# A Mamba layer on Trainium2: decays leave PSUM two pairs ahead, inputs stay there and are weighted in place, and the next image's norm is spread over five blocks

## The chip, the cores and the metric

The kernel runs on one core of one Trainium2 chip (trn2). The core has five engines with a queue each: PE (TensorE, the matmuls), ACT (ScalarE), DVE (VectorE), POOL (GpSimd) and SP (SyncE, which issues the DMAs here). Each engine takes its queue strictly in order; semaphores join the queues. The metric is the device time of one execution in microseconds (us). Three runs of the kernel before took 8034.1, 8043.04 and 8058.09 us, a median of 8043.04.

## What is computed

Four layers over `x` of 4 images, 56 x 56 positions, 128 channels, all in float32. Layer 0 is a neighbourhood attention, layer 2 an additive attention and a mixture of experts, layer 3 an attention and a second mixture of experts. The change is in layer 1, a group norm and two Mamba blocks in a row on each image row (a sequence of 56 steps):

```python
x = x + _L1_conv_ref(_gn(x), ...)          # _gn: mean and variance over 32 groups of an image

def _mamba_block(h, in_w, cw, cb, xw, dtw, dtb, A_log, Dp, ow):
    xz = h @ in_w                           # 128 -> 2 x 256
    u, res = jnp.split(xz, 2, axis=-1)
    u = silu(causal_conv(u, cw) + cb)       # 4 taps along the sequence
    dbl = u @ xw
    dt, Bm, Cm = jnp.split(dbl, [DT_RANK, DT_RANK + D_STATE], axis=-1)
    delta = softplus(dt @ dtw + dtb)
    A = -jnp.exp(A_log)
    y = _selective_scan(u, delta, A, Bm, Cm, Dp)
    return y * silu(res) @ ow

def _selective_scan(u, delta, A, Bm, Cm, Dp):
    deltaA = jnp.exp(jnp.einsum('btd,dn->btdn', delta, A))      # the decays
    deltaBu = jnp.einsum('btd,btn->btdn', delta * u, Bm)        # the inputs
    # h = deltaA[t] * h + deltaBu[t];  y[t] = sum over n of h * Cm[t]
    return y + u * Dp
```

There are 256 channels with 16 states each, so 4096 recurrences for each position.

## The kernel before, in words

**Blocks.** An image is cut into 7 chunks of 8 rows (448 positions). A block is one chunk in one of the two Mamba layers `l`; `order` lists 4 x 14 = 56 of them: for each image, chunks 0 to 3 in layer 0, then in layer 1, then chunks 4 to 6 in layer 0, then in layer 1. So the last block of an image that reads the normed image is its eleventh, and the next image's first block comes three blocks later.

**Pairs.** A block has 16 pairs. A pair is 2 x 8 channels x 16 states on 128 partitions, for 448 positions each: tiles of 128 x 896. For every pair the kernel does this:

- decays, `select`: two matmuls (PE, L654) spread `delta` times `A` into the PSUM tile `a` (two banks, two buffers); ACT takes the exponential in place (L668);
- inputs, `select` and `inputs`: two matmuls (PE, L663) spread `du` = delta * u into the PSUM tile `u` (two banks, one buffer). In 11 pairs of 16, DVE multiplies it by `Bm` (tile `bc`) into the SBUF tile `dBu` (L678). In the 5 pairs of `BY_POOL`, ACT copies it to SBUF (L672) and POOL multiplies it there (L673), since POOL has no access to PSUM;
- the recurrence, `scan`: one DVE scan instruction (L685) reads `a` (PSUM) and `dBu` (SBUF) and writes `hs` (SBUF, 7 buffers). The decay at the first position of each row is made 0 by a huge `delta`. POOL then multiplies `hs` by `Cm` (L690);
- `sums`, for two pairs at a time, five steps later: matmuls (PE, L696) add the states into the PSUM tile `y` (one bank), which began with `Dp * u` (`skip`, L704).

After 8 pairs `y` is complete for half the channels; `gate` multiplies it by silu(res) on DVE (L711). `project` (L720 or L728) is the output matmul, and `pass_on` (L738 on ACT for layer 0, L744 on DVE for layer 1) hands the result to the next layer or adds it to `X`.

**What prepares a block.** `mamba_pre` does the convolution, the projections, softplus and silu for the next block during the 16 steps of the current one. Its matmuls share one PSUM bank, `m`, with `project` and the norm. ACT changes its function table on the way from exp to silu and back, and from exp to softplus and back: four table loads for a block.

**The order** is written by hand. One step `p` issues, on all queues: the list `first[p]`, `select(p + 1)`, `scan(p)`, `sums` on odd steps, the list `last[p]`, and `inputs(p + 2)`. `select(p + 1)` issues on PE the decays of pair p+1 and then the inputs' matmuls of pair p+2. So a decay is made one step ahead of its scan and the weighted input two steps ahead. PE takes matmuls on different 32-row groups at the same time: decays use two of the groups of 32 partitions, the inputs' matmuls of the next pair the other two.

**The norm of the next image**, `prepare_image` from `group_norm_steps`: 7 steps that transpose a chunk (PE, L184), take its statistics (DVE, L187) and copy it to SBUF (ACT, L188), then `mean`, `var` and the normalising multiplies. Six of the chunks fall in three steps (11, 12, 13) of the block that is three before the image's first; the seventh, `mean`, `var` and all multiplies (L211) in steps 11 and 12 of the block after that.

**PSUM** has 8 banks: `m` 1, `a` 2 x 2, `u` 2, `y` 1.

Of the kernel before, what the change touches and what calls it, by code (L numbers as in the profile page):

```python
# [39 lines left out]

BY_POOL = (0, 3, 6, 9, 12)
# [65 lines left out]
class Hybrid:  # L107
# [61 lines left out]
    def group_norm_steps(self, b, pool, psum, group, pad=0):  # L169


        nc = self.nc
# [3 lines left out]
        def transposed(c):  # L176
            if c == 0:
                got["xn"] = self.t(pool, [P, HW, pad + HW], "xnT")
                got["st"] = self.t(pool, [P, NCH, nc.vector.BN_STATS_DIM], "gn_st")
                if pad:  # L180
                    nc.gpsimd.memset(got["xn"][:, :, 0:pad], 0.0)
            ps = psum()
            for k in range(TC):
                nc.tensor.transpose(  # L184
                    ps[:, k * TP : (k + 1) * TP], self.X[b][:, TC * c + k, :], self.ident[:TP, :TP]
                )
            nc.vector.bn_stats(got["st"][:, c, :], ps[:, :CH])  # L187
            nc.scalar.copy(chunk(c), ps[:, :CH].rearrange("p (s t) -> p s t", t=HW))  # L188

        def mean():  # L190
            mv = self.t(pool, [P, 2], "gn_mv")
            nc.vector.bn_aggr(mv, got["st"])
            pm = psum()
            nc.tensor.matmul(pm[:, 0:1], group, mv[:, 0:1], start=True, stop=True)
            got["mean"] = mean = self.t(pool, [P, 1], "gn_mean")
            nc.vector.tensor_copy(mean, pm[:, 0:1])
            got["dev"] = dev = self.t(pool, [P, 1], "gn_dev")
            nc.vector.tensor_sub(dev, mv[:, 0:1], mean)
            nc.vector.tensor_mul(dev, dev, dev)
            nc.vector.tensor_add(dev, dev, mv[:, 1:2])  # L200

        def var():
            pv = psum()
            nc.tensor.matmul(pv[:, 0:1], group, got["dev"], start=True, stop=True)
            var = self.t(pool, [P, 1], "gn_var")
            nc.vector.tensor_copy(var, pv[:, 0:1])
            got["r"] = self.rstd(pool, var, [P, 1], 1e-5, "gn")

        def normed(cs):
# [7 lines left out]
            [bind(transposed, c) for c in range(NCH)] + [mean, var]  # L217
            + [bind(normed, cs) for cs in (range(0, 2), range(2, 4), range(4, NCH))]
        )

# [104 lines left out]
    def layer0(self):  # L325
# [5 lines left out]
        with ExitStack() as ctx:  # L331
# [31 lines left out]
            def norm_steps(b):  # L363
                got, steps = self.group_norm_steps(b, big, m, group)
# [228 lines left out]
    def layer1(self):  # L593
# [5 lines left out]
        with ExitStack() as ctx:  # L599
# [5 lines left out]
            ps_a = ctx.enter_context(tc.tile_pool(name="l1_a", bufs=2, space=PSUM))  # L605
            ps_u = ctx.enter_context(tc.tile_pool(name="l1_u", bufs=1, space=PSUM))
# [14 lines left out]
            pre, yg, A, U, V, HS, py = {}, {}, {}, {}, {}, {}, {}  # L621

            def prepare_image(b):

                got, steps = self.group_norm_steps(b, big, m, w["group"], DC - 1)
# [5 lines left out]
                def rest():  # L631
                    for step in steps[NCH + 2 :]:
                        step()
                    hand_over()

                return steps[: NCH + 2] + [rest]
# [9 lines left out]


            def select(p):
                if 0 <= p < n_pairs:
                    j, f, q, r0 = place(p)  # L650
                    A[p] = two_banks(ps_a, "a")
                    for k in range(2):
                        own = slice((r0 + k) * HD, (r0 + k + 1) * HD)
                        nc.tensor.matmul(  # L654
                            halves(A[p])[:, k], w["A"][own, order[j][2], f, q, :], pre[j]["delta"][own, f],
                            start=True, stop=True,
                        )
                if p + 1 < n_pairs:
                    j, f, q, r0 = place(p + 1)
                    U[p + 1] = two_banks(ps_u, "u")  # L660
                    for k in range(2):
                        own = slice((r0 + k) * HD, (r0 + k + 1) * HD)
                        nc.tensor.matmul(  # L663
                            halves(U[p + 1])[:, k], w["pick"][own, q, :], pre[j]["du"][own, f],
                            start=True, stop=True,
                        )
                if 0 <= p < n_pairs:
                    nc.scalar.activation(A[p], A[p], AF.Exp)  # L668
                if p + 1 < n_pairs and (p + 1) % PAIRS in BY_POOL:
                    V[p + 1] = self.t(sm, [P, 2 * CH], "dBu", bufs=3)  # L670
                    v = halves(V[p + 1])
                    nc.scalar.copy(V[p + 1], U.pop(p + 1))  # L672
                    nc.gpsimd.tensor_mul(v, v, pre[j]["bc"][:, 0:1].to_broadcast([P, 2, CH]))  # L673

            def inputs(p):
                if p in U:
                    V[p] = self.t(sm, [P, 2 * CH], "dBu", bufs=3)
                    nc.vector.tensor_mul(  # L678
                        halves(V[p]), halves(U.pop(p)), pre[p // PAIRS]["bc"][:, 0:1].to_broadcast([P, 2, CH])
                    )  # L680


            def scan(p):
                flat = self.t(sm, [P, 2 * CH], "hs", bufs=7)
                nc.vector.tensor_tensor_scan(  # L685
                    flat, A.pop(p), V.pop(p), 0.0, op0=ALU.mult, op1=ALU.add
# [21 lines left out]
            def gate(j, f):  # L708
                if f == 0:
                    yg[j] = self.t(sm, [P, NHALF, CH], "yg", bufs=1)  # L710
                nc.vector.tensor_mul(yg[j][:, f], py.pop((j, f)), pre[j]["sres"][:, f])  # L711
# [38 lines left out]
            for j, block in enumerate(order):  # L750
                at = PAIRS * j
                if j and block[1:] == (0, 0):
                    for k, step in enumerate(prepare_image(block[0])):
# [1037 lines left out]
```

## Time and profile before

| what | us |
|---|---|
| median of three runs | 8043.04 |
| the profiled execution | 8038.93 |
| its span, first to last instruction | 8037.1 |
| layer 0 and the start, until the first scan | 637.4 |
| Mamba stage, first scan to start of the last | 637.4 to 3644.7 |
| layers 2 and 3 | about 3660 to 8037 |

Within the Mamba stage (the window 637 to 3646 us):

| group | count | mean ns | busy us |
|---|---|---|---|
| POOL `hs` times `Cm`, L690 | 895 | 2082 | 1840.0 |
| DVE scan, L685 | 896 | 2014 | 1795.2 |
| DVE `u` times `Bm`, L678 | 616 | 1078 | 664.0 |
| POOL `dBu` times `Bm`, L673 | 279 | 2084 | 581.3 |
| ACT exp, L668 | 896 | 906 | 811.3 |
| ACT copy of `u`, L672 | 279 | 911 | 254.1 |
| ACT table loads of L668, L804 and L835, four for a block | 225 | 1283 | 288.7 |
| DVE gate, L711 | 111 | 607 | 67.4 |

How to read a profile like this one: an engine's busy share over the whole span says little, since each layer has other limits; the window of the stage counts. A group's "idle before" is what its engine waited ahead of such an instruction, and the name behind the arrow is the instruction that ended the wait.

The starts of every sixteenth scan in the trace give the length of each block. 49 of the 55 blocks between the first and the last start of one last 52.3 us on average (49.6 to 53.6). The other six, the two ahead of the last block of each of the first three images, last 68.0 and 65.6 us: these are the ones with the norm of the next image in them.

### The profile page before, as it was taken

The page shows a single profiled execution, that of the slowest core. Times are in us where ns is not written, and L with a number is a line of the kernel's source. Part 1 is how long each engine was busy: PE and PEld are TensorE (multiplying, and loading weights), DVE is VectorE, ACT ScalarE, POOL GpSimd, SP SyncE. Part 2 cuts the span into 40 slices and gives each one's busy share as a digit, 9 for nine tenths or more (in the row PEclk, how much of TensorE's full clock was granted, in tenths as well). Part 3 has the DMA queues.
Part 4 walks back from the last instruction along what each step waited for, and adds up shares of the span by engine and source line. Part 5 has one row for each costly group of instructions (what it writes and reads, how often), then busy time and mean ns, then how long its engine had stood idle before and what let it go on. Part 6 is the DMA issues. An engine that isn't in the chain of part 4 may idle for free.

```text
span 8037.1 us, 106369 instructions
## 1 busy us (share of the span) xinstructions
PE 6835.5 (85%) x41037; PEld 2717.5 (34%) x41037; DVE 5818.5 (72%) x10093; ACT 5183.5 (64%) x5084; POOL 2975.3 (37%) x2077
## 2 busy tenths in 40 slices
PE   8878998999899999996777777777777779999999
PEld 4442333333333333332222222222222334444544
DVE  6777887888788888886777887887787764434434
ACT  4545565566565556655999899899989964333332
POOL 4547887888788888881000000000001000000000
PEclk9989998999899989998999899999989989999999
DMA  2000000000000000000000000000003101210000
GB/s 53 2 13 1 1 1 1 1 1 1 1 1 1 1 1 1 1 1 5 1 1 1 5 1 1 1 5 1 1 21 122 46 6 34 91 65 5 6 5 6
DMA packets 85494, 102.39 MB, mean 13 GB/s; under 512 B 21158, under 2 KB 50742, under 8 KB 84279
## 3 DMA queue, kind: packets, MB, share of 16 engines
q1 hardware_dynamic: 84985, 95.58, 4.0%
q8 instruction: 322, 5.28, 0.3%
q14 instruction: 187, 1.53, 0.1%
HBM read 85.28 MB, written 10.29 MB: 12 GB/s over the span
## 4 chain that ended last, share of the span: by engine, by line
PE 38%; ACT 17%; POOL 15%; issue 14%; DVE 10%; DMA 0%; SPq 0%; ACTq 0%; DVEq 0%; POOLq 0%
ACT th L1017 13%; POOL hs L690 10%; PE q L1563 7%; PE o L1574 7%; PE s L1028 6%; DVE th L1008 5%; POOL dBu L673 4%; PE o L1055 3%; PE a L654 2%; PE pe L1728 2%; PE m L792 2%; PE y L696 1%; PE u L663 1%; PE m L728 1%; POOL du L839 1%
## 5 line engine op out<-in xcount | busy, mean ns | idle before, releaser
L1017 ACT ACTIVATE th<-th 128x3136 f32<-128x3136 f32 (+12 forms) x1120 | 2294.2, 2094 | 202.5 <-DVE th L1008 147.7
L1008 DVE TENSOR_SCALAR th<-fT,g 128x784 f32<-128x784 f32 (+6 forms) x3920 | 1917.7, 556 | 492.1 <-PE s L1028 459.2
L1028 PE MATMUL s<-th,place 128*32 128x392 f32 (+7 forms) x14336 | 1488.1, 492 | 672.7 <-ACT th L1017 669.4
L685 DVE TENSOR_TENSOR_SCAN hs<-a,dBu 128x896 f32<-128x896 f32 x896 | 1795.2, 2014 | 274.5 <-ACT a L668 265.5
L690 POOL TENSOR_TENSOR hs<-hs,bc 128x896 f32<-128x896 f32 x896 | 1842.0, 2082 | 68.3 <-DVE hs L685 39.9
L668 ACT ACTIVATE a<-a 128x896 f32<-128x896 f32 x896 | 811.3, 906 | 790.7 <-PE u L663 604.9
L663 PE MATMUL u<-du,pick 32*128 32x448 f32 x3584 | 977.2, 619 | 96.8 <-ACT dBu L672 49.8
L654 PE MATMUL a<-delta,A_pick 32*128 32x448 f32 x3584 | 996.9, 605 | 7.0 <-DVE hs L685 6.1
L1028 PEld LDWEIGHTS s<-th,place 128*32 128x32 f32 (+1 forms) x14336 | 425.9, 111 | 1617.1 <-ACT th L1017 1089.5
L1046 POOL TENSOR_TENSOR e<-e,later 112x112 f32<-112x112 f32 x112 | 79.3, 708 | 2320.7 <-ACT e L1039 1680.8
L1568 ACT ACTIVATE e<-q,shift 128x448 f32<-128x448 f32 (+1 forms) x700 | 441.5, 634 | 729.8 <-PE q L1563 729.2
L678 DVE TENSOR_TENSOR dBu<-u,bc 128x896 f32<-128x896 f32 x616 | 664.0, 1078 | 164.6 <-PE u L663 163.4
L673 POOL TENSOR_TENSOR dBu<-dBu,bc 128x896 f32<-128x896 f32 x280 | 583.4, 2083 | 421.3 <-ACT dBu L672 421.2
L1574 PE MATMUL o<-e,xk 128*128 128x448 f32 (+1 forms) x1400 | 653.7, 549 | 25.7 <-ACT oT L1549 25.7
L1563 PE MATMUL q<-xT 128*128 128x448 f32 (+1 forms) x1400 | 653.8, 549 | 6.0 <-ACT e L1568 5.9
L1733 DVE SCALAR_TENSOR_TENSOR X<-pe,r_gate,X 112x128 f32<-112x128 f32 x896 | 314.1, 351 | 454.4 <-PE pe L1728 418.9
L654 PEld LDWEIGHTS a<-delta,A_pick 32*128 32x128 f32 x3584 | 313.7, 191 | 534.7 <-issue 246.2
L696 PE MATMUL y<-hs,sum 128*32 128x448 f32 x3584 | 446.8, 570 | 3.1 <-POOL hs L690 3.1
L1055 PE MATMUL o<-e,xa 112*128 112x392 f32 (+5 forms) x1024 | 427.5, 540 | 1.1 <-POOL e L1046 1.1
L663 PEld LDWEIGHTS u<-du,pick 32*128 32x128 f32 x3584 | 282.3, 191 | 331.1 <-DVE dBu L678 201.5
L1574 PEld LDWEIGHTS o<-e,xk 128*128 128x128 f32 (+1 forms) x1400 | 262.6, 191 | 310.0 <-issue 275.0
L1662 POOL MEMSET lc_xa<- 112x4 f32 x28 | 3.1, 110 | 893.2 <-DVE lc_xa L1656 625.8
(252 smaller groups left out, 7670.7 us busy)
## 6 DMA issues: line engine op xcount, KB each, us to landing
wide<-in_L_ffn_weight SPq DMA_DIRECT2D x64, 1024.0 KB
X<-in_x SPq DMA_DIRECT2D x8, 784.0 KB
out<-X SPq DMA_DIRECT2D x28, 224.0 KB
M<-wide SPq DMA_DIRECT2D x4, 784.0 KB
wide<-M SPq DMA_DIRECT2D x4, 784.0 KB
e_edge<-dtab SPq DMA_DIRECT2D x42, 49.0 KB
cw<-in_L_conv_conv_w SPq DMA_DIRECT2D x1, 1024.0 KB
c_h<-in_L_ffn_weight SPq DMA_DIRECT2D x16, 64.0 KB
```

The costliest lines, as they stand in the source:

```text
L654: nc.tensor.matmul(halves(A[p])[:, k], w["A"][own, order[j][2], f, q, :], pre[j]["delta"][own, f], start=True, stop=True,)
L663: nc.tensor.matmul(halves(U[p + 1])[:, k], w["pick"][own, q, :], pre[j]["du"][own, f], start=True, stop=True,)
L668: nc.scalar.activation(A[p], A[p], AF.Exp)
L673: nc.gpsimd.tensor_mul(v, v, pre[j]["bc"][:, 0:1].to_broadcast([P, 2, CH]))
L685: nc.vector.tensor_tensor_scan(flat, A.pop(p), V.pop(p), 0.0, op0=ALU.mult, op1=ALU.add)
L690: nc.gpsimd.tensor_mul(HS[p], HS[p], bc[:, 1:2].to_broadcast([P, 2, CH]))
L1008: nc.vector.tensor_scalar(th[i][:, blk, lo:hi], fT[j][:, lo:hi], im[order[j][0]]["g"][:, at : at + 1], None, op0=ALU.add,)
L1017: nc.scalar.activation(own, own, AF.Tanh)
L1028: nc.tensor.matmul(ps[j, J][QW * blk : QW * blk + rows, h, lo:hi], place[:, off : off + rows], z[:, blk, h * HALF + lo : h * HALF + hi], s ...
L1055: nc.tensor.matmul(po[j][:, h, lo:hi], im[b]["xa"][:, J, :], e[:, h * HALF + lo : h * HALF + hi], start=(J == 0), stop=(J == t + ((h + 1) ...
L1563: nc.tensor.matmul(ps[:n, :CH], xT[b][:, k : k + n], xT[b][:, c * CH : (c + 1) * CH], start=True, stop=True,)
L1574: nc.tensor.matmul(po[b, c], xk[b][:n, t, :], es.pop((b, c, t))[:n], start=(t == 0), stop=(t == N - 1))
```

## The change

- PSUM: `a` gets one buffer in place of two, `u` two in place of one.
- The decays are made two steps ahead: `select(p)` issues the decays of pair p+1 and the inputs' matmuls of pair p (each a pair later or earlier than before in the order). The exponential writes a new SBUF tile `E` (three buffers) and no longer works in place.
- The inputs stay in PSUM: DVE multiplies `u` by `Bm` in place, for all 16 pairs, one step ahead of the scan instead of two. `BY_POOL`, ACT's copy and POOL's multiply are gone, and so is `dBu`. The scan reads `E` from SBUF and `u` from PSUM.
- The gate becomes an ACT copy of `y` to SBUF and a POOL multiply; the first half is one step earlier, the second half at the end of step 3 and not at the start of step 4.
- `pass_on` moves from the start of its step (ahead of the scan) to the end.
- The norm of the next image: chunks in steps 11, 12, 13 of the blocks five and four before the image's first block, the seventh in step 11 of the third before; transposes at the end of a step, statistics and copy at the start of the next. Mean, variance and root are cut into six parts over steps 12 to 14 of the third block before, the multiplies in three parts and the handing over in steps 3, 5, 7 and 9 of the second. One DVE copy (of the variance) is gone. Layer 0 takes the same parts put together again as before.

```diff
-            ps_a = ctx.enter_context(tc.tile_pool(name="l1_a", bufs=2, space=PSUM))
-            ps_u = ctx.enter_context(tc.tile_pool(name="l1_u", bufs=1, space=PSUM))
+            ps_a = ctx.enter_context(tc.tile_pool(name="l1_a", bufs=1, space=PSUM))
+            ps_u = ctx.enter_context(tc.tile_pool(name="l1_u", bufs=2, space=PSUM))
...
+            def decays(p, to):
+                j, f, q, r0 = place(p)
+                for k in range(2):
+                    own = slice((r0 + k) * HD, (r0 + k + 1) * HD)
+                    nc.tensor.matmul(
+                        halves(to)[:, k], w["A"][own, order[j][2], f, q, :], pre[j]["delta"][own, f],
+                        start=True, stop=True,
+                    )
...
             def select(p):
+                if 0 <= p + 1 < n_pairs:
+                    t = two_banks(ps_a, "a")
+                    decays(p + 1, t)
                 if 0 <= p < n_pairs:
...
+                    V[p] = two_banks(ps_u, "u")
+                    spread_inputs(p, V[p])
+                if 0 <= p + 1 < n_pairs:
+                    E[p + 1] = self.t(sm, [P, 2 * CH], "E", bufs=3)
+                    nc.scalar.activation(E[p + 1], t, AF.Exp)
+
+            def inputs(p):
                 if 0 <= p < n_pairs:
-                    nc.scalar.activation(A[p], A[p], AF.Exp)
-                if p + 1 < n_pairs and (p + 1) % PAIRS in BY_POOL:
-                    V[p + 1] = self.t(sm, [P, 2 * CH], "dBu", bufs=3)
-                    v = halves(V[p + 1])
-                    nc.scalar.copy(V[p + 1], U.pop(p + 1))
-                    nc.gpsimd.tensor_mul(v, v, pre[j]["bc"][:, 0:1].to_broadcast([P, 2, CH]))
-
-            def inputs(p):
-                if p in U:
-                    V[p] = self.t(sm, [P, 2 * CH], "dBu", bufs=3)
+                    v = halves(V[p])
                     nc.vector.tensor_mul(
-                        halves(V[p]), halves(U.pop(p)), pre[p // PAIRS]["bc"][:, 0:1].to_broadcast([P, 2, CH])
+                        v, v, pre[p // PAIRS]["bc"][:, 0:1].to_broadcast([P, 2, CH])
                     )
...
-                    flat, A.pop(p), V.pop(p), 0.0, op0=ALU.mult, op1=ALU.add
+                    flat, E.pop(p), V.pop(p), 0.0, op0=ALU.mult, op1=ALU.add
...
-                nc.vector.tensor_mul(yg[j][:, f], py.pop((j, f)), pre[j]["sres"][:, f])
+                nc.scalar.copy(yg[j][:, f], py.pop((j, f)))
+                nc.gpsimd.tensor_mul(yg[j][:, f], yg[j][:, f], pre[j]["sres"][:, f])
...
-                    for k, step in enumerate(prepare_image(block[0])):
-                        add(last, at - (3 if k < 6 else 2) * PAIRS + 11 + k % 6 // 2, step)
-                add(last, at + 12, gate, j, 0)
-                add(first, at + PAIRS + 4, gate, j, 1)
+                    chunks, stats, norms = prepare_image(block[0])
+                    for k, (turn, take) in enumerate(chunks):
+                        to = at - (5 - k // 3) * PAIRS + 11 + k % 3
+                        add(last, to, turn)
+                        add(first, to + 1, take)
+                    to = at - 3 * PAIRS + 12
+                    for k, (where, step) in enumerate(zip((first, last) * 3, stats)):
+                        add(where, to + k // 2, step)
+                    for k, step in enumerate(norms):
+                        add(last, at - 2 * PAIRS + 3 + 2 * k, step)
+                add(last, at + 11, gate, j, 0)
+                add(last, at + PAIRS + 3, gate, j, 1)
                 add(last, at + PAIRS + 8, project, j)
-                add(first, at + PAIRS + 9, pass_on, j)
+                add(last, at + PAIRS + 9, pass_on, j)
...
-                inputs(p + 2)
+                inputs(p + 1)
```

In step p the order of the queues is now: `first[p]`; on PE the decays of pair p+2 and the inputs' matmuls of pair p+1; on ACT the exponential of pair p+2; on DVE `scan(p)`; `sums`; `last[p]`; on DVE the multiply of pair p+1.

## The prediction

> **What bounds the kernel now.** I read the slices of the span first, for the stage; then the stage's chain of waits; then its groups; then the engine sums of single blocks.
>
> The page's slices, 201 us each; slices 4 to 19 are the Mamba stage:
>
> ```profile
> PE   8878998999899999996777777777777779999999
> DVE  6777887888788888886777887887787764434434
> ACT  4545565566565556655999899899989964333332
> POOL 4547887888788888881000000000001000000000
> ```
>
> Three engines stand at 8 to 9 tenths and none is full, so waits between queues matter as much as any engine's sum. The change touches nothing that issues a DMA. The groups:
>
> ```profile
> L685 DVE TENSOR_TENSOR_SCAN hs<-a,dBu 128x896 f32<-128x896 f32 x896 | 1795.2, 2014 | 274.5 <-ACT a L668 265.5
> L690 POOL TENSOR_TENSOR hs<-hs,bc 128x896 f32<-128x896 f32 x896 | 1842.0, 2082 | 68.3 <-DVE hs L685 39.9
> L668 ACT ACTIVATE a<-a 128x896 f32<-128x896 f32 x896 | 811.3, 906 | 790.7 <-PE u L663 604.9
> L678 DVE TENSOR_TENSOR dBu<-u,bc 128x896 f32<-128x896 f32 x616 | 664.0, 1078 | 164.6 <-PE u L663 163.4
> ```
>
> POOL is busiest of the three where it works (16 x 2.08 + 5 x 2.08 + 2.08 = 45.8 us of a block of 52.3 us) and hardly waits; in the chain of this stage it holds 27.1% by L690 and 11.4% by L673. The scan's idle time is nearly all waiting for the exponential: the decay is made one step ahead, and each table change delays it. A plain block and one with the next image's norm (engine sums):
>
> ```profile
> 750.00:801.00 51.00, 46.60 (x236) 15.41 (x232) 43.43 (x30) 31.28 (x39) 44.94 (x26) 0.97 0.00 1
> 1260.00:1311.00 51.00, 47.31 (x219) 18.17 (x218) 36.81 (x27) 28.77 (x35) 36.60 (x20) 0.86 0.00 1
> ```
>
> After the window come PE, PE's weight loads, DVE, ACT, POOL and the PE clock. In the second window DVE and POOL lose some 7 us each: PE's `m` bank passes from transposes to DVE to ACT and back, six times in three steps. The block starts give 52.3 us for a plain block and 66.8 us as the mean of the six with a norm.
>
> **What is removed.** POOL loses 5 x 2.08 us a block and gains two gate multiplies (half of 2.08 each): 37.5 us, no longer near a bound. ACT loses 5 x 0.91 and gains two copies of 0.54 (row L854): about 28 us, hidden. The chain that POOL leaves goes to DVE.
>
> **DVE's new floor.** It takes 5 more multiplies and loses two gates. How instructions follow each other, from two stretches of the timeline:
>
> ```profile
> 748.01 2.01 DVE L685 TENSOR_TENSOR_SCAN hs<-a,dBu 128x896 f32<-128x896 f32 x1
> 749.94 1.06 DVE L678 TENSOR_TENSOR dBu<-u,bc 128x896 f32<-128x896 f32 x1
> ```
>
> ```profile
> 466.05 1.54 DVE L465 RECIPROCAL d<-d 128x224 f32<-128x224 f32 x1
> 467.62 0.74 DVE L466 TENSOR_TENSOR oT<-oT,d 128x224 f32<-128x224 f32 x1
> ```
>
> The multiply does not need the scan before it and starts 1.93 us after that scan's start, 0.08 before its end. The second instruction below needs the first one's result, and starts 0.03 after its end. The new scan reads what the multiply just before it wrote, which the old order avoided. So a pair is 1.93 + 1.078 + 0.035 = 3.04 us (without that dependence 2.92). 896 x 3.04 = 2724 us. The adds to `X` (28 x 0.61) bring 17. The norms: seven statistics of 0.55, seven multiplies in 3.05 and eleven small operations of about 0.2 are 9.2 us an image, three images 28. The floor is 2769 us, against 3007 between the first and the last scan now.
>
> **The multiply's write to PSUM.** No DVE row here writes PSUM. From below: rows L678 (1078 ns for 896) and L711 (607 for 448) give 1.05 ns an element and 136 ns fixed; losing all of the fixed part would be -136 ns. From above: reading and writing one bank takes turns, as long as a scan, 2014 ns, +936. I take 1078 unchanged: ACT's exponential in place in PSUM (906 ns) and its copy of the same size from PSUM to SBUF (911) show no turns. The scan still reads one operand from each memory: 2014. Row L711 reads PSUM and takes 607 ns for 448 elements; row L1278, all in SBUF, takes 609. The Trainium skill (Perfetto Trace Analysis, Optimizing Scalar/DVE Operations) gives DVE about 60 ns of access overhead on SBUF and 125 on PSUM, which the two rows don't show for a read; if it held for the write, an estimate of 65 ns a pair or 58 us, the time would be some 8006 in place of 7948.
>
> **What keeps DVE from its floor.** I follow one block, with m the start of a step's multiply, 3.04 us apart. The inputs' matmuls of the next pair can start once the scan before m's has ended (m + 0.15) and take 1.0; they are due at m + 3.04, so PE may run 1.8 us late. But they stand behind the decays of the pair after on PE, and with one `a` buffer those wait for the previous exponential. The spots:
>
> ```profile
> 798.23 0.90 ACT L668 ACTIVATE a<-a 128x896 f32<-128x896 f32 x1 [0.33 <-PE u L663]
> 799.15 1.28 ACT L804 ACT_TABLE_LOAD   x1
> 800.44 0.95 ACT L804 ACTIVATE sres<-raw_res 128x896 f32<-128x896 f32 x1
> 801.30 0.93 ACT L804 ACTIVATE us<-raw 128x896 f32<-128x896 f32 x1
> 802.25 1.28 ACT L668 ACT_TABLE_LOAD   x1
> 803.54 0.90 ACT L668 ACTIVATE a<-a 128x896 f32<-128x896 f32 x1
> ```
>
> - silu, step 2: 5.3 us from one exponential's start to the next's. Steps 15 to 1 load PE with convolutions (1.85 each) and `sums` (0.9), so exp(4) starts about 8.5 us after m(0), exp(5) ends at 14.7, decays(6) and inputs(5) at 15.8; multiply(5) was due at 15.2. Wait: 0.6.
> - softplus, step 6: its exponentials are 4.9 us apart (758.97 to 763.87 in the same view); in the same way multiply(9) comes 0.45 late.
> - `project` of the second layer's blocks: about 3.6 us on PE in step 8, then the inputs of pair 10: 1.5 late, of which the add to `X` fills 0.6. 0.9 in 28 blocks.
> - the square root's two table loads: about 1 us an image.
>
> Together 56 x 1.05 + 28 x 0.9 + 3 = 87 us. The last exponential of a step delays no scan by itself (two steps of lead are 6 us). `pass_on`, now behind the scan, holds `m` for the residual matmuls of step 9, which have slack there. The gate's copy on ACT frees `y` a step before `skip` needs it, where PE now waits 1 to 2 us for DVE.
>
> **The clock.** The trace's clock records halve PE's clock in stretches of 3.4 us or more, on a grid of 3.41 us; a block at 0.97 holds one. Nearly all halved stretches follow a grid window whose matmuls covered 55 to 73%: about 1 us of waiting is enough. In my walk PE waits 1.2 us for silu and 2 us around softplus, so one or two patches come in each block, each taking up to 1.7 us from PE, part of it inside the slack. Bounds: 0 and 3.4 us a block. I take 1.0: 56 us. The Trainium skill (TensorE: Matmul & The Clock Gate, Part 1) has the clock fall after a whole idle window; by that rule the 56 us drop out and the time is 7892, but the records above show it at a quarter idle, so I keep them.
>
> **Sum.** 2769 + 87 + 56 = 2912 for 3007: 95 us less. The profiled execution took 8038.9, so 7944; the median of the runs is 4 us above it: 7948. Of this the norm's blocks give 6 x (66.8 - 52.3) - 28 = 59, the plain blocks the other 36. What stands before the first scan and after the last is left as it is.
>
> **Rivals.**
> - *Packed*: PE is early enough everywhere and the clock costs nothing: 2769, which is 238 less: 7805. For it: a lead of two steps and 1.8 us of slack. Against: the walk, with its late inputs behind one `a` buffer.
> - *PE sets the pace* (slower): decays and inputs behind one `a` buffer turn each table change into a late multiply, and the halved clock falls on both spots and on `project`: 56 x 3.4 + 28 x 1.7 = 238 us in place of 56, so 3094, 87 more: 8130. It decides from 2.7 us of clock a block (3007 reached). For it: PE's 46.6 us busy of 51 are highest of all. Against: up to half of them are decays and inputs one after the other that run together when both are ready.
> - *The write takes turns* (slower): with +936 ns, a pair is 3.98 us, the waits vanish under it, 3566 + 45 = 3611: 8647. Decides from about 110 to 200 ns a multiply. Against: the ACT rows.
> - *Nothing to see*: the plain blocks lose as much as the norm's gain, 2.3 to 3.1 us of clock a block.
>
> **How the numbers follow.** The forecast (7870 to 8019) 0.55, packed 0.15, nothing 0.10, PE's pace 0.15, turns 0.05. A measurement of this kernel can tell some 0.3%, 24 us, from no change: faster 0.70, same 0.10, slower 0.20. The range cuts half of packed and most of the slow cases' far side: 7830 to 8090.
>
> **What would show it.** The multiply's row near 1078 ns; scan starts 3.04 us apart in steps 11 to 15 and waits before the multiplies of steps 5, 9 and 10 named after PE's `u`; no block above 56 us; POOL near 38 us a block; DVE first in the chain. I am wrong if the multiply's row grows, if those waits add to over 5 us a block, or if ACT's exponential still ends the scans' waits.

## The result, and the profile after

The changed kernel takes 7935.08 us (median; 7930.36 to 7940.73), the one before 8042.46 beside it: a ratio of 0.9865, 95% interval 0.9847 to 0.9882. That is 107 us less, where 95 were forecast. The profiled execution has a span of 7928.6 us, 108.5 less than before; from the first scan's start to the last one's it is 2893.2 us in place of 3007.4. So the whole gain lies in the Mamba stage. Outside it the profiled execution is some 6 us longer, which says nothing: over the thirteen profiled kernels of this case, whose work there is all but the same, that time goes from 5028 to 5045 us.

The page's slices after, 198 us each; the stage now runs from slice 4 into slice 18:

```profile
PE   8878988998899899977777777777777889999999
DVE  6777999999999999986877787887787755344434
ACT  4445555555555555537998899899889964333332
POOL 4545776777777677760000000000001000000000
```

DVE stands at 9 in slices 5 to 17, where three engines shared 7s to 9s before. POOL has fallen to 6 and 7. The page's groups of the stage (busy us, mean ns of one, then the idle time just before them with what ended it):

```profile
L713 POOL TENSOR_TENSOR hs<-hs,bc 128x896 f32<-128x896 f32 x896 | 1868.2, 2085 | 798.8 <-DVE hs L708 772.7
L708 DVE TENSOR_TENSOR_SCAN hs<-E,u 128x896 f32<-128x896 f32 x896 | 1810.0, 2020 | 115.8 <-DVE u L701 2.0
L696 ACT ACTIVATE E<-a 128x896 f32<-128x896 f32 x896 | 821.5, 917 | 805.9 <-PE u L680 332.7
L701 DVE TENSOR_TENSOR u<-u,bc 128x896 f32<-128x896 f32 x896 | 963.8, 1076 | 48.0 <-PE u L680 47.9
```

Three things are to be read here. The multiply that now reads and writes PSUM costs 1076 ns, what it cost into SBUF (1078). No scan waits for an exponential any more. And the scan still has 115.8 us of idle time of which only 2.0 carry a name: 0.13 us ahead of every one of 896 scans, with nothing that the view can blame. POOL's long idle time costs nothing: it waits for scans. One number must not be read as it stands, the multiply's 47.9 us of waiting for PE. The view of waits gives it as sum, times and longest:

```profile
DVE u L701 <- PE u L680: 47.9, 35, 34.6
```

The longest, 34.6 us, lies ahead of the stage's first multiply, when the first block is being prepared. Within the stage the multiplies wait 13.2 us for PE, in 34 waits.

A plain block and one with the next image's norm, as engine sums (window, PE, weight loads, DVE, ACT, POOL, then the PE clock):

```profile
751.00:802.00 51.00, 46.46 (x232) 15.39 (x232) 48.42 (x33) 28.73 (x36) 37.74 (x23) 0.97 0.00 1
1250.00:1301.00 51.00, 43.55 (x213) 16.40 (x214) 48.89 (x38) 25.79 (x32) 29.14 (x18) 0.85 0.00 1
```

In the norm's block DVE is now as full as in a plain one. By the starts of every sixteenth scan a plain block lasts 51.00 us on average (52.26 before), and each of the two ahead of an image's last block 57.72 (66.81 before). So plain blocks gave 55 x 1.26 = 69 us and the norm's excess 6 x (14.55 - 6.72) = 47; the fifteen pairs behind the start of the last block took 2 back, which leaves the 114 of the stage. The stage's chain of waits, before and after:

```profile
by line: POOL hs L690 27.1%; issue 22.1%; POOL dBu L673 11.4%; PE a L654 6.6%; PE m L792 5.3%; PE y L696 3.3%; PE u L663 2.8%; POOL du L839 2.1%; PE m L728 2.1%; DVE hs L685 2.0%; PE y L704 1.8%; DVE dBu L678 1.6%; PE m L810 1.6%; PE m L821
```

```profile
by line: DVE hs L708 51.5%; DVE u L701 20.4%; ACT E L696 5.9%; issue 3.6%; PE a L671 3.3%; ACT L696 2.0%; ACT delta L869 1.5%; PE m L744 1.5%; PE m L826 1.4%; DVEq L708 1.1%; PE y L719 0.8%; POOL hs L713 0.8%; PE u L680 0.7%; DVE xnT L226 0
```

Scan and multiply hold 72% of it; POOL's products, 38% before, hold 0.8%. `DVEq L708`, DVE's own queue ahead of the scan, is new in the list (1.1%) and leads to the surprise of this case. The timeline of DVE in steps without a table change (start, duration, then the instruction):

```profile
714.70 2.02 DVE L708 TENSOR_TENSOR_SCAN hs<-E,u 128x896 f32<-128x896 f32 x1
716.64 1.07 DVE L701 TENSOR_TENSOR u<-u,bc 128x896 f32<-128x896 f32 x1
717.85 2.02 DVE L708 TENSOR_TENSOR_SCAN hs<-E,u 128x896 f32<-128x896 f32 x1
720.16 1.10 DVE L701 TENSOR_TENSOR u<-u,bc 128x896 f32<-128x896 f32 x1 [0.30 <-PE u L680]
721.40 2.02 DVE L708 TENSOR_TENSOR_SCAN hs<-E,u 128x896 f32<-128x896 f32 x1
```

From scan to scan it is 3.15 us at 714.70; the median at 15 of the 16 places in a block is 3.14, where 3.04 was forecast. A multiply starts 0.08 before the end of the scan ahead of it, as forecast, but the scan starts 0.14 after its multiply's end by these rounded lines, not 0.035. Over the stage the median of this gap is 0.132. The sixteenth place, from scan 9 to scan 10 (counted from 0), is longer: 3.74 in the median. The add to `X` (0.67 us) stands there in every second block or so, and nearly all of the late multiplies.

So the total came out near the forecast, yet the pace was missed: 896 x 0.097 = 87 us too slow. Something else must have been overpriced by more. The experiments look for both.

### The profile page after: what moved, and what is told of

Read it like the earlier page. It is cut to its first block, busy times and chain, and to the rows that moved or that the text cites. A ratio compares the mean times of both kernels' runs of the same rounds, so it can differ in the third digit from the quotient of the medians.

```text
span 7928.6 us, 105809 instructions
## 1 busy us (share of the span) xinstructions
PE 6709.2 (85%) x41037; PEld 2666.4 (34%) x41037; DVE 6087.8 (77%) x10253; ACT 5017.8 (63%) x4916; POOL 2551.3 (32%) x1909
## 4 chain that ended last, share of the span: by engine, by line
DVE 35%; PE 32%; ACT 19%; issue 7%; POOL 1%; DVEq 0%; DMA 0%; SPq 0%; ACTq 0%; POOLq 0%
DVE hs L708 19%; ACT th L1051 13%; DVE u L701 7%; PE q L1597 7%; PE o L1608 7%; PE s L1062 6%; DVE th L1042 5%; PE o L1089 3%; PE pe L1762 2%; ACT E L696 2%; PE a L671 1%; ACT L696 1%; PE m L826 1%; DVE e L455 1%; ACT e L1073 1%
## 5 line engine op out<-in xcount | busy, mean ns | idle before, releaser
L713 POOL TENSOR_TENSOR hs<-hs,bc 128x896 f32<-128x896 f32 x896 | 1868.2, 2085 | 798.8 <-DVE hs L708 772.7
L708 DVE TENSOR_TENSOR_SCAN hs<-E,u 128x896 f32<-128x896 f32 x896 | 1810.0, 2020 | 115.8 <-DVE u L701 2.0
L696 ACT ACTIVATE E<-a 128x896 f32<-128x896 f32 x896 | 821.5, 917 | 805.9 <-PE u L680 332.7
L701 DVE TENSOR_TENSOR u<-u,bc 128x896 f32<-128x896 f32 x896 | 963.8, 1076 | 48.0 <-PE u L680 47.9
L671 PEld LDWEIGHTS a<-delta,A_pick 32*128 32x128 f32 x3584 | 296.5, 188 | 699.1 <-ACT E L696 468.5
L1597 PEld LDWEIGHTS q<-xT 128*128 128x128 f32 (+1 forms) x1400 | 248.7, 189 | 243.6 <-issue 211.8
```

The source lines that it names most:

```text
L671: nc.tensor.matmul(halves(to)[:, k], w["A"][own, order[j][2], f, q, :], pre[j]["delta"][own, f], start=True, stop=True,)
L696: nc.scalar.activation(E[p + 1], t, AF.Exp)
L701: nc.vector.tensor_mul(v, v, pre[p // PAIRS]["bc"][:, 0:1].to_broadcast([P, 2, CH]))
L708: nc.vector.tensor_tensor_scan(flat, E.pop(p), V.pop(p), 0.0, op0=ALU.mult, op1=ALU.add)
L713: nc.gpsimd.tensor_mul(HS[p], HS[p], bc[:, 1:2].to_broadcast([P, 2, CH]))
L1597: nc.tensor.matmul(ps[:n, :CH], xT[b][:, k : k + n], xT[b][:, c * CH : (c + 1) * CH], start=True, stop=True,)
```

## The experiments

All changes are against the changed kernel, unless said; ratios are to the kernel before, with their 95% intervals.

### What stands in the 0.13 us

The view of a single line lists the queue's own semaphore instructions beside the operation. The scan after:

```profile
L708 DVEq EVENT_SEMAPHORE  x896: 21/50/50, 638.8 to 3532.0; - x180
L708 DVE TENSOR_TENSOR_SCAN hs<-E,u x896: 1959/2021/2023, 638.8 to 3532.1; 128x896 f32<-128x896 f32 x180
```

Each scan waits for three things: its multiply on DVE, ACT's exponential and, for the buffer of `hs`, POOL's product of seven pairs earlier. An extra semaphore instruction of 50 ns (minimum 21, median 50) stands in the queue before it for that. Since it takes part of the waiting, and the multiply before it is what the scan waits for last, it runs in the gap. In the trace it starts 38 ns behind the multiply's end, lasts 50, and the scan starts 44 ns behind its end (medians), together 132. The theory: the gap is the price of those waits; the rivals are PSUM (the scan reads a bank that DVE has just written) and the plain dependence.

**`early`**: the multiply, whose own waiting falls under the scan ahead of it, takes the waits for ACT and POOL; the scan keeps the one for DVE. The work is the same.

```diff
-                    nc.scalar.activation(E[p + 1], t, AF.Exp)
+                    made[p + 1] = nc.scalar.activation(E[p + 1], t, AF.Exp)
...
-                    nc.vector.tensor_mul(
+                    of = nc.vector.tensor_mul(
...
+                    for other in (made.pop(p), shown.pop(p - 7, None)):
+                        if other is not None:
+                            tc.add_manual_dep(
+                                of.ins, other.ins.name,
+                                mybir.DependencyInfo(mybir.DependencyClass.Sync, mybir.DependencyReason.DATA),
...
-                nc.gpsimd.tensor_mul(HS[p], HS[p], bc[:, 1:2].to_broadcast([P, 2, CH]))
+                shown[p] = nc.gpsimd.tensor_mul(HS[p], HS[p], bc[:, 1:2].to_broadcast([P, 2, CH]))
```

> In the changed kernel the scan starts 0.13 us after the multiply it depends on ends; the prediction had 0.035. Theory A: the scan carries three waits (DVE, ACT, POOL), and two of them stand in an instruction of their own of 0.05 us that runs only when the multiply is done. Here the multiply carries the waits for ACT and POOL, the scan only that for DVE: the gap falls to about 0.035, a pair of scans to 3.04 us, and the stage gets up to 896 x 0.095 = 85 us shorter: 7850, or up to 7910 if the late multiplies that the prediction named (1.05 us a block) come back at the faster pace. Theory B: the gap is the multiply's write to PSUM that takes longer to be acknowledged: it stays at 0.10 or more and the time stays at 7935.

Measured: 7896.73 us, 0.9812 (0.9796 to 0.9829). DVE's timeline:

```profile
759.48 1.07 DVE L701 TENSOR_TENSOR u<-u,bc 128x896 f32<-128x896 f32 x1
760.59 2.02 DVE L715 TENSOR_TENSOR_SCAN hs<-E,u 128x896 f32<-128x896 f32 x1
762.52 1.07 DVE L701 TENSOR_TENSOR u<-u,bc 128x896 f32<-128x896 f32 x1
763.63 2.02 DVE L715 TENSOR_TENSOR_SCAN hs<-E,u 128x896 f32<-128x896 f32 x1
```

and the line of its multiply:

```profile
L701 DVEq EVENT_SEMAPHORE  x896: 21/50/50, 636.6 to 3500.3; - x180
  PE u L680: 88.3, 125
```

The semaphore instruction has moved to the multiply, where the scan ahead covers it. The gap is 0.034 us and the median pace 3.05 (3.04 in these lines), where the prediction had 3.04. The dependence and the bank are the same as before, so neither makes the gap; it is the price of the scan's waits. The stage's time fell by less than the gap's 87 us: 2893.2 to 2865.4, 28 us. The waits say why:

```profile
DVE u L701 <- PE u L680: 88.3, 125, 31.9
```

The longest again lies ahead of the stage. Within it the multiplies wait 56 us for PE's inputs in place of 13. The other 16 or so are overlap with the scan ahead, which a late multiply loses, and the multiplies themselves (1080 ns for 1076, and each starts 5 ns later). So at the slower pace the gap had covered a good part of PE's lateness.

**`to_sbuf`**: the multiply writes an SBUF tile, and the scan reads both operands there. It asks whether the gap is PSUM's.

```diff
-                    v = halves(V[p])
+                    u, V[p] = V[p], self.t(sm, [P, 2 * CH], "dBu", bufs=3)
                     nc.vector.tensor_mul(
-                        v, v, pre[p // PAIRS]["bc"][:, 0:1].to_broadcast([P, 2, CH])
+                        halves(V[p]), halves(u), pre[p // PAIRS]["bc"][:, 0:1].to_broadcast([P, 2, CH])
                     )
```

> The changed kernel with one edit: the multiply writes its product to a tile in SBUF and no longer in place in PSUM; the scan then reads both operands from SBUF. Theory A (the waits in front of the scan): the gap between multiply and scan stays 0.13 us, the multiply stays at 1.08 and the scan at 2.02, time 7935 within 20. Theory B (the write to PSUM): the gap falls to 0.035 to 0.065, 60 to 85 us less. Theory C (two operands in SBUF get in the way of POOL, which reads SBUF all the time): the scan's 2.02 or POOL's 2.085 us grow; if they took turns, a pair would be 4.1 us or more and the time about 8790.

Measured: 8667.3 us, 1.0774 (1.0755 to 1.0793), 9% over the changed kernel. Its groups in the window 637 to 3500 us, four fifths of its stage:

```profile
L713 POOL TENSOR_TENSOR hs<-hs,bc 128x896 f32<-128x896 f32 x703 | 2330.9, 3343 | 145.6 <-DVE hs L708 131.4 <-PE a L671 8.1 <-PE u L680 4.0
L708 DVE TENSOR_TENSOR_SCAN hs<-E,dBu 128x896 f32<-128x896 f32 x706 | 1960.3, 2777 | 90.8 <-DVE dBu L701 1.0 <-ACT E L696 0.5
L701 DVE TENSOR_TENSOR dBu<-u,bc 128x896 f32<-128x896 f32 x705 | 748.0, 1061 | 31.3 <-PE u L680 31.1
```

The gap stays (90.8 us over 706 scans, 0.13), so it is not PSUM's. The multiply is only 15 ns cheaper into SBUF. What costs 732 us is new: the scan rises from 2020 to 2777 ns and POOL's product from 2085 to 3343, both at once. With two operands in SBUF the scan and POOL get in each other's way. How they do it stands in the timeline of the two engines:

```profile
748.45 2.64 DVE L708 TENSOR_TENSOR_SCAN hs<-E,dBu 128x896 f32<-128x896 f32 x1
749.18 3.79 POOL L713 TENSOR_TENSOR hs<-hs,bc 128x896 f32<-128x896 f32 x1
752.21 2.65 DVE L708 TENSOR_TENSOR_SCAN hs<-E,dBu 128x896 f32<-128x896 f32 x1
```

The first scan ends at 751.09, POOL's product 1.88 us later at 752.97, the next scan 1.89 behind that at 754.86. They take turns: an instruction that starts while the other runs ends as if it had begun at the other's end. All 849 scans of this run that last over 2.3 us end 1.877 to 1.888 us behind the end of the POOL instruction that they ran into, and all 676 products over 2.4 us end 1.866 to 1.897 behind their scan.

**`two_ahead`**: the same with the product in SBUF, but made two steps ahead of its scan, the decays three, with four buffers for `E`. Nothing that the scan needs is then fresh.

```diff
-                    decays(p + 1, t)
-                if 0 <= p < n_pairs:
-                    V[p] = two_banks(ps_u, "u")
-                    spread_inputs(p, V[p])
+                    decays(p + 2, t)
...
+                    V[p + 1] = two_banks(ps_u, "u")
+                    spread_inputs(p + 1, V[p + 1])
+                if 0 <= p + 2 < n_pairs:
+                    E[p + 2] = self.t(sm, [P, 2 * CH], "E", bufs=4)
+                    nc.scalar.activation(E[p + 2], t, AF.Exp)
...
-                inputs(p + 1)
+                inputs(p + 2)
```

> The multiply writes to SBUF and runs two pairs ahead of its scan, the decays three ahead. No scan needs the instruction just before it, so by theory A the gap is gone: scan and multiply overlap by 0.085 each, 2.92 us a pair, DVE 47.0 us a block; PE's 46.5 us a block would be next, some 48 to 49 a block in all: 7790 to 7850. By theory C the scans or POOL's multiplies grow and it is slower than 7935.

Measured: 8661.74 us, 1.0764 (1.0748 to 1.0780). The gap is gone (no idle time before scans), and the pace is the same 3.76 us as in `to_sbuf`: the scan takes 2787 ns, POOL's product 3422 (window 637 to 3500 us). The turns set the pace, 1.88 + 1.88 us, and taking the gap away gains nothing.

**`no_pool`**: `to_sbuf` without POOL's product of `hs` and `Cm`, to see whether the collision is with that instruction.

```diff
-                bc = pre[p // PAIRS]["bc"]
-                nc.gpsimd.tensor_mul(HS[p], HS[p], bc[:, 1:2].to_broadcast([P, 2, CH]))
```

> The run whose multiply writes to SBUF, without POOL's multiply of hs by Cm, which is left out. There the scan took 2.78 us with both operands in SBUF and POOL's multiply 3.34, for 2.02 and 2.085 in the changed kernel. If the two get in each other's way, the scan is back at 2.02; if a scan with two operands in SBUF is slow by itself, it stays at 2.78.

Measured, one run: 7958.88 us. The scan's group in the window 637 to 3500 us:

```profile
L708 DVE TENSOR_TENSOR_SCAN hs<-E,dBu 128x896 f32<-128x896 f32 x878 | 1862.8, 2122 | 88.7 <-DVE dBu L701 1.4 <-ACT E L696 0.5
```

The median scan is 2025 ns again and the pace 3.11 us. The mean of 2122 holds the scans that met POOL's other work (`du`, the gate). So the collision is shown by taking away one of the two. The run also gives a third point for the gap: without POOL's product the scan waits for two things, its extra semaphore instruction takes 21 ns in place of 50, and the gap is 0.103 in place of 0.132.

### What the prediction had overpriced: PE's lateness

**`lead_less`**: two buffers for `E` in place of three, so that the exponential of pair p+1 waits for the scan of p-1. This takes back the second step of lead.

```diff
-                    E[p + 1] = self.t(sm, [P, 2 * CH], "E", bufs=3)
+                    E[p + 1] = self.t(sm, [P, 2 * CH], "E", bufs=2)
```

> The changed kernel with two E tiles in place of three: the exponential of pair p+2 now waits for the end of scan p, not of scan p-1, so that the decays lead by one pair less; nothing else differs. If the lead is what took the waits out of the scans, the table changes are back: exp(4) starts a pair later, multiply(5) and multiply(9) come 1 to 2 us later in each block, 2 to 3 us a block, 110 to 170 us in all: 8045 to 8105. If DVE's own work alone sets the pace, the time stays within 25 of 7935.

Measured: 8116.31 us, 1.0090 (1.0075 to 1.0105): slower than the kernel before, and 11 us beyond the range expected. Waits, longest sums first (us in total, times, longest):

```profile
PEld a L671 <- ACT E L696: 1016.1, 737, 4.7
ACT E L696 <- DVE hs L708: 1000.4, 584, 4.3
...
DVE u L701 <- PE u L680: 208.8, 182, 32.1
```

The chain reads from the middle: ACT waits for the scan, PE's decays wait for ACT since `a` has one buffer, the inputs behind them on PE come late, and the multiply waits (177 us within the stage, 13 in the changed kernel). The median from scan 4 to scan 5 is 4.49 us, from scan 8 to scan 9 4.91, from 9 to 10 4.08 and from 10 to 11 3.41, against 3.14 elsewhere; a plain block lasts 54.5 us. Scan 4 to 5 and 8 to 9 lie two steps behind the table changes for silu (step 2) and softplus (step 6), where the prediction's walk put its waits. So the mechanism exists, and the third `E` buffer removes most of it: 181 us.

**`inputs_first`**: `early`, with PE issuing the inputs' matmuls ahead of the decays.

```diff
-                if 0 <= p + 1 < n_pairs:
-                    t = two_banks(ps_a, "a")
-                    decays(p + 1, t)
                 if 0 <= p < n_pairs:
                     V[p] = two_banks(ps_u, "u")
                     spread_inputs(p, V[p])
                 if 0 <= p + 1 < n_pairs:
+                    t = two_banks(ps_a, "a")
+                    decays(p + 1, t)
```

> The run with the early waits, and PE's two pairs of matmuls of a step exchanged: first the inputs' (they wait for a scan), then the decays' (they wait for an exponential). With the early waits a plain block takes 50.5 us for 16 x 3.05 = 48.8, and the scans' starts are 0.3 to 0.8 us too far apart after pairs 4 and 9. If those are inputs' matmuls that stand behind decays that wait for a late exponential, they go: 49.0 to 49.4 a block, 60 to 85 us less than 7897: 7815 to 7840. If PE is simply too busy there, nothing changes: 7880 to 7900.

Measured: 7897.84 us, 0.9817 (0.9803 to 0.9832), no better than `early`. By place it did half of what it should: the medians behind scans 4 and 8, 3.34 and 3.10 in `early`, are 3.05. But behind scan 9 it grew from 3.84 to 4.12, and behind scan 10 from 3.08 to 3.47. What stands there, from the timeline of its engines:

```profile
718.65 0.53 ACT L769 COPY h<-m 128x448 f32<-128x448 f32 x1
719.23 1.02 PE L887 MATMUL m<-xnT,res_w 128*128 128x448 f32 x2 [0.65 <-ACT h L769]
...
721.35 1.10 DVE L701 TENSOR_TENSOR u<-u,bc 128x896 f32<-128x896 f32 x1 [0.31 <-PE a L671]
```

`pass_on`'s copy frees `m` late; PE's residual matmuls wait for it, and the inputs stand behind them.

**`best`**: `inputs_first`, with `pass_on` back at the start of its step for blocks of Mamba layer 0, so that ACT's copy is not behind an exponential.

```diff
-                add(last, at + PAIRS + 9, pass_on, j)
+                add(last if block[2] else first, at + PAIRS + 9, pass_on, j)
```

> The run with the early waits and the inputs first, and for blocks of the first Mamba layer pass_on's copy ahead of the exponential of its step again. With the inputs first the waits after pairs 4 and 8 are gone, but those after 9 grew to 1.2 us: the residual matmuls wait for that copy, and the inputs' matmuls stand behind them. If the copy is the cause, half of that goes in 28 blocks: 7865 to 7885. If PE's load in steps 8 to 10 is, it stays at 7890 to 7900.

Measured: 7874.94 us, 0.9794 (0.9780 to 0.9809), under both kernels. From the first to the last scan it takes 2844.8 us (`early` 2865.4); by the ratios it is 15 us under `early`, with intervals that touch. A plain block lasts 50.1 us. The time is in the range that was expected if the copy is the cause, but the waits are not gone where that range had them: behind scan 9 the median is still 4.12, and DVE's waits there fall only from 47 us in `inputs_first` to 41, those behind scan 10 from 12 to 4. The multiply's group shows what is left:

```profile
L701 DVE TENSOR_TENSOR u<-u,bc 128x896 f32<-128x896 f32 x896 | 964.8, 1077 | 71.2 <-PE a L671 62.5 <-POOL h L768 6.0 <-PE u L680 2.2
```

Of the 71.2 us, 38 lie within the stage (the rest ahead of its first multiply), most of them named after the decays that PE now issues last. Which of the works in front of them on PE is at fault was not separated.

### What the other parts of the change are worth

**`gate_dve`**: the gate as one DVE multiply again, at its new place.

```diff
-                nc.scalar.copy(yg[j][:, f], py.pop((j, f)))
-                nc.gpsimd.tensor_mul(yg[j][:, f], yg[j][:, f], pre[j]["sres"][:, f])
+                nc.vector.tensor_mul(yg[j][:, f], py.pop((j, f)), pre[j]["sres"][:, f])
```

> The changed kernel with the gate as one DVE multiply again, in its new place. DVE is busy 48.4 of 51 us in a plain block: if its work sets the pace, two gates of 0.52 us a block are added almost in full, 50 to 60 us: 7985 to 7995. If the waits around steps 5 and 9 or PE set the pace, they vanish in these and the time stays within 20 of 7935.

Measured: 8000.27 us, 0.9944 (0.9927 to 0.9960), 65 over the changed kernel. 112 gates of 607 ns are 68: on this full DVE an instruction costs its own duration. It shows in place as well: the medians behind scans 3 and 11 are 3.67 and not 3.14.

**`coarse_norm`**: the norm's steps bunched in their old steps.

```diff
-                    for k, (turn, take) in enumerate(chunks):
...
-                        add(last, at - 2 * PAIRS + 3 + 2 * k, step)
+                    steps = [list(fs) for fs in chunks] + [stats[:3], stats[3:], norms]
+                    for k, fs in enumerate(steps):
+                        for step in fs:
+                            add(last, at - (3 if k < 6 else 2) * PAIRS + 11 + k % 6 // 2, step)
```

> The changed kernel with the next image's norm put back where it was, six chunks in three steps and the rest in two. In the changed kernel the two blocks with most of the norm take 55 and 59 us for 50.9, some 13 us an image; before they took 29 us more than a plain block. If the fine steps are what saved this, the six blocks take 66 us again and the time is 45 to 55 us longer: 7980 to 7990. If the decays' lead of two pairs hides a bunched norm just as well, it is less than 15 us longer.

Measured: 7936.46 us, 0.9865 (0.9850 to 0.9879): the same as the changed kernel. The norm's blocks last 59.55 us against 57.72, and the plain ones make up for part of it (50.89 against 51.00). One reason why the fine steps pay so little is a cost of their own. The norm's multiplies, in `after` and then here:

```profile
L226 DVE TENSOR_SCALAR xnT<-xnT,gn_mean,gn_r 128x448 f32<-128x448 f32 x21 | 25.3, 1254 | 0.0
L226 DVE TENSOR_SCALAR xnT<-xnT,gn_mean,gn_r 128x448 f32<-128x448 f32 x21 | 9.2, 508 | 0.1
```

Spread over the steps, nine of the 21 run into a product of POOL and last 2.27 us in place of 0.49. All the norm's instructions together keep DVE busy for 52 us of the stage with the fine steps and for 36 here, so the fine steps give back 16 us of the waiting that they save.

**`lead_less_coarse`**: both `lead_less` and `coarse_norm`, to see whether the fine steps matter where the lead is missing.

> Both edits at once: two E tiles (8116 alone) and the next image's norm in its old, bunched place (7936 alone, no more than the changed kernel). If the lead of the decays is what hides a bunched norm, then without it the norm costs again what it cost before, some 15 us more for an image: 8155 to 8170. If the fine steps never mattered, it stays at 8105 to 8125.

Measured: 8155.88 us, 1.0144 (1.0127 to 1.0161), 40 over `lead_less`; the norm's blocks last 65.1 us, not far from the 66.8 of the kernel before, against 59.0. So the fine steps are worth 40 us without the lead and 1 with it: most of the waiting that they save, the lead saves too.

**`before_all_dve`**: the kernel before, with all 16 multiplies on DVE.

```diff
-BY_POOL = (0, 3, 6, 9, 12)
+BY_POOL = ()
```

> The kernel before with one edit: no pair goes to POOL, DVE multiplies all 16 into SBUF. POOL falls to 35 us a block, DVE rises from 42.8 to 47.8 us of work. If POOL's chain (38% of the stage's chain of waits) is what held the kernel before, it gets faster, 8000 or less. If it is the decays' short lead, the scans still wait for the exponentials and DVE has 5 us a block less to spare: 8060 to 8250.

Measured: 8068.44 us, 1.0033 (1.0020 to 1.0046), 25 slower. Ten of the 16 medians are 2.91 or 2.92, the pace that the prediction gave for a pair without the dependence, and 5.24 us stand behind scan 3 and 3.6 and 3.5 behind scans 7 and 8. Behind scans 3 and 7 the next scan starts late by 129 us in all, and nearly always 0.09 us behind the end of its own exponential (the view of waits names POOL's product for most of them, which had ended before the exponential). So taking work from POOL pays nothing here while the exponential is one step ahead.

## Why the prediction was right

It said 2912 us from the first scan to the last; it is 2893. That the total came so near is luck: three of its terms were wrong, two too low and one far too high. From the trace the stage is 896 x 3.14 = 2813 for the pairs, 18 for the adds to `X`, 52 for the norm's instructions on DVE and 13 of waiting for PE, 2896 in all, a few too many since neighbours overlap. The prediction's terms were 2724, 17, 28 and 87 + 56 = 143.

- **The dependence** is a step that failed. "The second instruction below needs the first one's result, and starts 0.03 after its end" was read off an instruction that waits for that one alone, and put on a scan with three waits. It measured 0.132 in place of 0.035, 87 us. `early` shows that the 0.035 was right for a scan with a single wait.
- **The norm's instructions on DVE** were put at 28 us (seven multiplies in 3.05 for an image, small operations at about 0.2 each), and are 52: beside POOL's products some of them take 1 to 2 us longer (`coarse_norm`).
- **What keeps DVE from its floor and the clock** were put at 143 us; the multiplies wait 13 within the stage. This follows in part from the first error: at 3.14 a pair each late input has 0.1 us a pair more to catch up. At the pace that the walk used (`early`) the waits are 56, and they stand where the walk named them, ahead of the multiplies of pairs 5, 9 and 10: behind scans 4, 8 and 9 DVE waits 15, 9 and 24 us in all, for 34, 25 and 25 in the walk, and 8 more behind scan 10. So its mechanism and places were right at its own pace; silu and softplus were put at two to three times what they cost. The 56 us for the clock were a term of their own, while the 56 that were measured hold whatever the clock adds to them; how much that is the runs do not tell. By the clock records PE is halved for 474 us of the stage before, 215 after and 225 in `early`. The prediction's "about 1 us of waiting is enough" to bring such a stretch does not hold after: of 69 grid windows of the stage that matmuls covered to 70 to 75%, 3 were followed by a halved one.
- **The norm's blocks give 59**: 47 by the block starts. The size was near, but steps spread over five blocks are not what brings it: with the lead, the spreading is worth 1 us (`coarse_norm`).
- **The plain blocks' 36** came out at 69: the gap took 87 and the waits that did not come gave 130, shared with the norm's blocks.
- **The multiply's write to PSUM** was taken at 1078 ns and is 1076; the scan taken at 2014 is 2020. The rival in which the write takes turns (8647) falls. For the same multiply, rows into PSUM and into SBUF now exist: 1076, against 1061 in `to_sbuf` and 1078 in the kernel before. The Trainium skill (Perfetto Trace Analysis, Optimizing Scalar/DVE Operations) gives about 60 ns of overhead on SBUF and 125 on PSUM, 65 between the two; these rows show 15 at most.
- **POOL** near 38 us a block: 37.7. **DVE first in the chain**: yes. **No block above 56**: wrong, the norm's blocks last 55 to 60, since DVE itself is full there and the norm's instructions come on top. **Scan starts 3.04 us apart and waits ahead of multiplies 5, 9 and 10**: neither in the changed kernel, where the pace is 3.14 and nearly all waits stand behind scans 9 and 10; both in `early`.
- **Packed** (7805) falls: `best`, with 38 us of the multiplies' waits left, is still 70 us above it. **PE sets the pace** (8130) falls for this kernel, but `lead_less` shows how near it was: with one buffer less it is 8116. **Nothing to see** falls by the interval.

The gain of 107 us therefore needs the lead and DVE's relief from the gate: without the third `E` buffer the change loses some 70 us to the kernel before, and without the gate's move only some 45 are left. Moving POOL's five multiplies alone loses 25. No run has the lead with those five still on POOL, so whether that move is needed for the gain is not shown.

## What to carry to other kernels

When an instruction is put right behind the one that feeds it, count its other waits too: let the feeding instruction, or an earlier one on the same queue, take those for engines that were done long ago, so that the dependent one waits for one thing. When the bounding engine speeds up, rework the waits of the others at the new pace; a slow pace hides lateness, and a gain in pace is given back in part (here 87 us of gap brought 28). Take a sum of waits apart before using it: one wait ahead of the stage made 35 of the 48 us here. And before two edits that shorten the same wait are both made, try each without the other: a lead of one more step had made the fine steps all but worthless.

## What the hardware showed

- From the end of one DVE instruction to the start of the next it is -0.08 us (multiply behind a scan that it does not need), +0.034 (scan that needs the multiply, one wait), +0.103 (two waits, with a semaphore instruction of 21 ns in the queue, `no_pool`) or +0.132 (three waits, with one of 50 ns). The last is 38 ns to the semaphore instruction, 50 in it and 44 behind it.
- A scan with one operand in PSUM runs beside POOL's products at full speed (2020 and 2085 ns); with both operands in SBUF the two take 2777 and 3343. The Trainium skill (SBUF — State Buffer, Who interferes with whom) has a DVE instruction with two SBUF inputs contend, for an exclusive lock, with a GpSimd instruction that reads SBUF. The trace of `to_sbuf` agrees: scan and product alternate, each ending 1.88 us behind the other. That makes the pace of 3.76 us, less than the 2.02 + 2.09 = 4.11 of the two one after the other, since the first 0.14 us of a scan and 0.2 of a product pass while the other still runs. That `u` stays in PSUM is what keeps this change from it.
- A small instruction can be caught as well: in the changed kernel L220, a product of two 128 x 1 tiles in the norm, takes 1951 ns beside POOL's product and 160 in `coarse_norm`.
